# Moving the output norm of a Mamba chunk, and the start of the MLP woven into it

## The chip, the cores and the metric

The kernel runs on one core of one Trainium2 chip. The metric is the time of one execution on the device in microseconds; lower is better. The core's engines work side by side, each through its own queue of instructions in order: TensorE (PE, matrix products; PEld is its loading of weights), VectorE (DVE), ScalarE (ACT, which also evaluates functions such as exp, sqrt and silu), GpSimd (POOL) and SyncE (SP, which here issues most transfers). They meet through semaphores.

## The reference, cut to what matters

One layer for 2048 tokens of width 512, in float32: a Mamba2 mixer and a gated MLP, then a mixture of eight experts, two for each token.

```python
def mamba2(x, ...):
    z, xb, Bc, Cc, dt = split(x @ in_proj_w)
    xBC = silu(causal_depthwise_conv(cat(xb, Bc, Cc), conv_w, conv_b))
    y = ssd_chunked(x_h * dt, dt * A, B_h, C_h) + D * x_h    # chunks of 128 tokens
    y = rmsnorm(y * silu(z), norm_w)
    return y @ out_proj_w

def attn(hidden):
    h = hidden + mamba2(rmsnorm(hidden, ln1_w), ...)
    h2 = rmsnorm(h, ln2_w)
    return h + silu(h2 @ gate_w) * (h2 @ up_w) @ down_w

x = x + attn(layernorm(x))
x = x + experts(layernorm(x))      # top 2 of 8, weighted
```

## The kernel before

**Tiling.** The 2048 tokens are cut into 16 chunks of 128 (index `t`), 8 blocks `b` of two chunks, and 4 MLP blocks `fb` of two blocks each. Tokens stand on the partitions where a norm is taken, features where a product follows; `transposed` (L182) turns a tile with four PE transposes `pt` and one DVE product that reads them out (L190).

**Mamba.** `mamba(b)` (L784) is a generator: it does the two chunks of block `b` and, between their steps, what block `b+1` needs (`prepare`, and `project`: in-projection halves `pm` and `pz` of L312, convolution, silu). It yields 16 times in a chunk, 32 times in a block. `chunk(b, j, ...)` (L366) is a generator too, of which `mamba` takes eight steps in each chunk, and a ninth at the chunk's end (`yield "end"`, then `finish(pieces)`). For each half `gp` of the heads it multiplies `ec` by the channels on POOL (L378), takes scores `psc` (L383), exponentials of `cum` on ACT (L389), their products on DVE (L391), sums `py` (L406 and L414) in the only buffer of pool `ps_y`, and the new state (L421, L436). The tile `xd` (L397, one buffer) is written by DVE in the first half. `cum` comes by a broadcast transfer (L284, SP) and is masked on POOL (L286) in `spread`; `ec` by transfers of L296.

The end of a chunk is what the change touches. In step 6, `y` is squared on ACT into `sq` (L449, L450), which shares `xd`'s buffer, and summed on POOL (L452). In step 7, PE projects `y` into `po` (L457, 8 matmuls, pool `ps_mm` of two buffers), and sums the squares over the partitions (`pms`, L459). Then come the root and reciprocal `ry` (L141, L142), the normed input plus the projection `h` (L464, L465, DVE), the residual `x += h` on POOL (L466) and its store on ACT's queue (L467). The next `x` loads (L78) wait for such stores. Two empty yields follow. The ninth part squares `h` into a new tile with the sum in `m2` (L473), takes the root `r2`, multiplies (L476) and transposes the result into `h2T[fb]`, the MLP's input.

**MLP.** `feed_forward(fb)` (L670) works on 512 tokens as two halves, with seven products in place of eight: `sums` (L651) forms sums `ts` of the halves of `h2T` (L657 to L660). Each of 16 column blocks `c` has four pieces of two products `px`, `py` (L683) and two matmul groups of an earlier pair's down-projection `pd` (L667, added up by DVE in L668). ACT copies products out of PSUM (L722, L728, L735), DVE adds others (L710, L716, L742, L747), silu is in L711 and L717. A 65th piece does the last down-projections; then `route` (L550) normalises and picks experts.

**Order.** PE's instructions are placed by a tile scheduler, by priority, in blocks 0 and 1; from block 2 on they run as written. The other engines' are scheduled throughout. The driver (L833 to L854) starts the generator of `feed_forward(fb-1)` with block `2*fb` and takes one piece of it at each piece of Mamba, the 65th at the `"end"` of the second block, and a step of routing at every fourth piece. The last MLP block (`fb = 3`) runs after Mamba, and the experts last.

Of the kernel before, what the change touches and what calls it, by code (L numbers as in the profile page):

```python
# [8 lines left out]
F32 = mybir.dt.float32  # L9
I32 = mybir.dt.int32  # L10
AF = mybir.ActivationFunctionType
ALU = mybir.AluOpType
# [3 lines left out]
P = 128  # L16
T = 2048
D = 512
NK = D // P
# [5 lines left out]
NCH = TB // P  # L25
NB = T // TB
FB = 512
NFB = T // FB
# [3 lines left out]
NFC = DFF // FC  # L32
# [12 lines left out]
C_CW, C_CB, C_NW, C_D, C_L1, C_L2, C_DTB, C_AL = 0, 48, 60, 68, 76, 80, 84, 100  # L45
# [4 lines left out]
def mamba_mlp_moe(ctx, tc, x, w_in, w_out, w_gu, w_down, par, wr, wg, wu, wd, out):  # L50
# [3 lines left out]
    nc = tc.nc  # L54

    def bc(ap, axis, n):
        ap = ap.unsqueeze(axis)
        shape = list(ap.shape)
        shape[axis] = n
        return ap.to_broadcast(shape)  # L60
# [19 lines left out]
    params = pw.tile([P, NPAR], F32, name="params")  # L80
# [58 lines left out]
    def rsqrt_eps(dst, src, scale=1.0):  # L139

        nc.scalar.activation(dst, src, AF.Sqrt, bias=eps, scale=scale)  # L141
        nc.vector.reciprocal(dst, dst)  # L142
# [12 lines left out]
    wa = pa_stack.enter_context(tc.tile_pool(name="wa", bufs=2))  # L155
# [7 lines left out]
    ps_mm = psa_stack.enter_context(tc.tile_pool(name="ps_mm", bufs=2, space=PSUM))  # L163
    ps_sg = psa_stack.enter_context(tc.tile_pool(name="ps_sg", bufs=1, space=PSUM))
    ps_y = psa_stack.enter_context(tc.tile_pool(name="ps_y", bufs=1, space=PSUM))
# [3 lines left out]
    def bank(kind, shape, name):  # L169
        pool, tag = use[kind]  # L170
        return pool.tile([P, *shape], F32, name=name, tag=tag)
# [10 lines left out]
    def transposed(src, dst, weight=None):  # L182

        pt = bank("tr", [NK, P], "pt")
        for k in range(NK):
            nc.tensor.transpose(pt[:, k, :], src[:, k * P : (k + 1) * P], ident)  # L186
        if weight is None:
            nc.scalar.copy(dst, pt)
        else:
            nc.vector.tensor_tensor(dst, pt, bc(weight, 2, P), ALU.mult)  # L190
# [108 lines left out]
    def finish(steps):  # L299
        while True:  # L300
            try:
                next(steps)
            except StopIteration as end:
                return end.value
# [42 lines left out]
    def channels(b):  # L347
        xb = wa.tile([P, 4, TB], F32, name=f"xb{b}", tag="xb")
        return xb, [None, None]

    state = wa.tile([P, 2, 4, HD], F32, name="state", bufs=1)
    h2T = [None] * NFB

    def turned_x(t, xb):

        tok = slice(t % NCH * P, (t % NCH + 1) * P)
        pt = ps_tr.tile([P, 4, P], F32, name=f"ptx{t}", tag="tr")
        for m in range(4):
            nc.tensor.transpose(pt[:, m, :], xb[:, m, tok], ident)
        xbt = wa.tile([P, 2, 4, HD], F32, name=f"xbt{t}", tag="xbt")  # L360
        nc.scalar.copy(xbt.rearrange("p a g d -> p (a g d)"), pt.rearrange("p a q -> p (a q)"))
        return xbt
# [3 lines left out]
    def chunk(b, j, dt, ncum, dtdec, cd, cum, ec, xb, cs, zs):  # L366

        t = b * NCH + j
        tok = slice(j * P, (j + 1) * P)
# [3 lines left out]
        y = zs[:, :, tok]  # L373

        for gp in range(2):
# [49 lines left out]
            for i in range(4):  # L425
                at = C_D + 4 * gp + i
# [19 lines left out]
            xbts[t + 1] = turned_x(t + 1, xb if j == 0 else xc[0])  # L446

        sq = wa.tile([P, 8, P], F32, name=f"sq{t}", tag="xd", bufs=1)
        nc.scalar.activation(sq[:, 0:4, :], y[:, 0:4, :], AF.Square)  # L449
        nc.scalar.activation(sq[:, 4:8, :], y[:, 4:8, :], AF.Square)  # L450
        for n in (4, 2, 1):
            nc.gpsimd.tensor_tensor(sq[:, 0:n, :], sq[:, 0:n, :], sq[:, n : 2 * n, :], ALU.add)  # L452
        yield

        po = ps_mm.tile([P, D], F32, name=f"po{t}", tag="mm")
        for m in range(8):
            nc.tensor.matmul(po, y[:, m, :], w_o[:, m, :], start=(m == 0), stop=(m == 7))  # L457
        pms = ps_tr.tile([P, 1], F32, name=f"pms{t}", tag="tr")
        nc.tensor.matmul(pms, sq[:, 0, :], ones[:, 0:1], start=True, stop=True)  # L459

# [2 lines left out]
        h = wa.tile([P, D], F32, name=f"h{t}", tag="tok", bufs=3)  # L463
# [1 line left out]
        nc.vector.scalar_tensor_tensor(h, po, ry, h, ALU.mult, ALU.add)  # L465
        nc.gpsimd.tensor_tensor(res[t], res[t], h, ALU.add)  # L466
        nc.scalar.dma_start(out=resd[t], in_=res[t])  # L467
        yield
        yield

        h2 = wa.tile([P, D], F32, name=f"h2{t}", tag="tok", bufs=3)
        m2 = wa.tile([P, 1], F32, name=f"m2{t}", tag="m2")
        nc.scalar.activation(h2, h, AF.Square, accum_out=m2)  # L473
        r2 = wa.tile([P, 1], F32, name=f"r2{t}", tag="r2")
        rsqrt_eps(r2, m2, scale=1.0 / D)
        nc.vector.tensor_scalar_mul(h2, h, r2)  # L476
        fb, off = divmod(t * P, FB)
        if off == 0:
            h2T[fb] = (wk if fb % 2 else wa).tile([P, 2, NK, FH], F32, name=f"h2T{fb}", tag="h2T", bufs=1)
        half, off = divmod(off, FH)  # L480
        transposed(h2, h2T[fb][:, half, :, off : off + P], params[:, C_L2 : C_L2 + NK])

# [1 line left out]


    KH = NK // 2
    AT_ONCE = 400
    early_d = [scratch.tile([P, 3, KH, FC], F32, name=f"early{c}", tag=f"early{c}") for c in range(NFC)]  # L490
    late_d = [scratch.tile([P, 4, KH, FC], F32, name=f"late{c}", tag=f"late{c}") for c in range(NFC)]

# [177 lines left out]
    def feed_forward(fb):  # L670
# [20 lines left out]
        for c in range(NFC):  # L691
# [15 lines left out]
            def p2():  # L707
                product(x2, late[:, 2], b21)
                with tc.high_priority(AT_ONCE):
                    nc.vector.tensor_tensor(a[:, 0], a[:, 0], x2, ALU.add)  # L710
                nc.scalar.activation(a[:, 0], a[:, 0], AF.Silu)  # L711

            def p3():
                product(x2, late[:, 1], b22, False)
                with tc.high_priority(AT_ONCE):
                    nc.vector.tensor_tensor(a[:, 1], a[:, 1], x2, ALU.add)  # L716
                nc.scalar.activation(a[:, 1], a[:, 1], AF.Silu)  # L717

            def p5():
                product(x2, early[:, 1], t1)  # L720
                with tc.high_priority(AT_ONCE):
                    nc.scalar.copy(up, x2)  # L722
# [3 lines left out]
            product(x1, early[:, 0], b11)  # L726
            with tc.high_priority(AT_ONCE):
                nc.scalar.copy(a[:, 0], x1)  # L728
# [4 lines left out]
            product(x1, early[:, 2], t2, False)  # L733
            with tc.high_priority(AT_ONCE):
                nc.scalar.copy(a[:, 1], x1)  # L735
# [4 lines left out]
            product(x1, late[:, 0], t3, False)  # L740
            with tc.high_priority(AT_ONCE):
                nc.vector.tensor_tensor(up, up, x1, ALU.add)  # L742
# [27 lines left out]
    xc = channels(0)  # L770
    ready = None
    for pair in range(6):
# [3 lines left out]
        elif pair == 2:  # L776
            ready = finish(coming)
# [5 lines left out]

    def mamba(b):  # L784

        nonlocal ready, xc
        hT, dt, ncum, dtdec, cd, _ = ready
        xb, cs = xc
        zs = wa.tile([P, 8, TB], F32, name=f"zs{b}", tag="zs", bufs=1)
        if b + 2 < NB:  # L790
            load_x((b + 2) * NCH)
        more = b + 1 < NB
        if more:
            coming = prepare(b + 1)
            xc = channels(b + 1)
        n = 0
        for j in range(NCH):
            pieces = chunk(b, j, dt, ncum, dtdec, cd, *near[j], xb, cs, zs)
            for _ in range(4):

                if n < 2:
                    halves = (gate(b, pair, hT, zs) for pair in (2 * n, 2 * n + 1))
                elif more:
                    halves = project(b + 1, n - 2, next_hT, *xc)
                else:
                    halves = iter(())
                next(pieces)
                if more and n == 0:
                    next(coming)
                yield  # L810
                next(pieces)
                if more and n == 3:
                    next(coming)
                next(halves, None)
                yield
                if more and n < 3:
                    next(coming)
                elif more and n == 3:
                    ready = finish(coming)
                next(halves, None)  # L820
                yield
                if more and n == 0:
                    next_hT = next(coming)
                yield
                n += 1
            yield "end"
            finish(pieces)
            if j == 0 and b + 2 < NB:
                load_x((b + 2) * NCH + 1)
            if more:  # L830
                near[j] = spread(b + 1, j, ready[-1])

    BPF = FB // TB  # L833
    tail = None
    in_order = ExitStack()
    for fb in range(NFB):
        if fb == 1:

            in_order.enter_context(tc.manual_schedule(engines={mybir.EngineType.PE}))
        feed = feed_forward(fb - 1) if fb else None  # L840
        for b in range(fb * BPF, (fb + 1) * BPF):
            n = 0
            for piece in mamba(b):
                if piece == "end":
                    if feed and b % BPF == BPF - 1 and n == 16 * NCH:
                        next(feed)
                    continue
                n += 1
                if feed:
                    next(feed)  # L850
                if tail and n % 4 == 3:
                    next(tail, None)
        tail = feed
    pa_stack.close()  # L854


# [87 lines left out]
    feed = feed_forward(NFB - 1)  # L944
# [8 lines left out]
    tail = routed(tail)  # L953
# [181 lines left out]
```

## Time and profile before

| | us |
|---|---|
| runs, median (lowest to highest) | 1606.52 (1604.34 to 1612.76) |
| profiled execution | 1616.04 |
| its span, first to last instruction | 1614.1 |
| PE busy in it | 1549.4 |
| ACT table loads in it, 195 of 1.283 us | 250.2 |

The stages lie thus in the span: block 0's inputs until about 80 us, the chunks of blocks 0 and 1 without an MLP until about 216, Mamba and MLP woven together until about 1090, the last MLP until about 1255, then the experts. A row of the profile names line, engine, operation, the tile written, an arrow and the tiles read, with partitions x elements; in a timeline the brackets at the end tell how long the engine had been idle and what ended that. One fp32 matmul of the program is two records of the trace, two passes.

### The profile page before, as it was taken

To read this page: it belongs to the slowest core of one execution; us is meant where nothing else is said; L and a number is where in the kernel's file an instruction comes from. 1 tells how busy PE (TensorE), PEld (TensorE's weight loads), DVE (VectorE), ACT (ScalarE), POOL (GpSimd) and SP (SyncE) were. 2 spreads that over 40 slices of the span, in tenths; PEclk is the share of its full clock that TensorE was granted. 3 is DMA by queue.
4 is the path that set the end of the run, shared out by engine and by line. 5 is a ranking of instruction groups with operands and counts; after the bars stand their busy time and mean duration, and the time that the engine had idled before them with its cause. 6 is when DMAs were issued, how large, how long until landed. Compare 5 with 4: busy or idle time off the path is not lost. (4 is left out here: it accounts for less than half of the span.)

```text
span 1614.1 us, 18988 instructions
## 1 busy us (share of the span) xinstructions
PE 1549.4 (96%) x6283; PEld 1057.4 (66%) x6283; DVE 766.1 (47%) x2019; ACT 679.9 (42%) x1287; POOL 401.6 (25%) x486
## 2 busy tenths in 40 slices
PE   5998979999999999999999999998999999999997
PEld 4756567767676766777676677657666656666663
DVE  4785744554456557536554673444533352222221
ACT  3897875643553555246545443223122211111110
POOL 5222243342341112211221121011100113333331
PEclk9999989999999999999999999999999989999999
DMA  7553535554554543343454432237785223333332
GB/s 237 174 151 98 161 102 161 182 174 155 167 193 140 165 156 125 124 125 125 137 163 158 160 97 85 88 119 264 221 295 166 85 40 66 66 66 65 66 65 33
DMA packets 127326, 218.66 MB, mean 135 GB/s; under 512 B 11456, under 2 KB 71360, under 8 KB 127232
## 3 DMA queue, kind: packets, MB, share of 16 engines
q1 hardware_dynamic: 104960, 166.08, 33.1%
q0 software_dynamic: 8736, 20.45, 7.2%
q10 hardware_dynamic: 13536, 30.94, 5.1%
q8 instruction: 52, 0.85, 0.2%
q14 instruction: 42, 0.34, 0.1%
HBM read 176.01 MB, written 41.42 MB: 135 GB/s over the span
## 5 line engine op out<-in xcount | busy, mean ns | idle before, releaser
L667 PE MATMUL pd<-md,a 128*128 128x512 f32 x512 | 238.5, 592 | 0.0
L312 PE MATMUL pm<-hT,wi 128*128 128x256 f32 x768 | 190.9, 396 | 0.0
L312 PEld LDWEIGHTS pm<-hT,wi 128*128 128x128 f32 x768 | 147.8, 198 | 28.9 <-issue 6.9
L667 PEld LDWEIGHTS pd<-md,a 128*128 128x128 f32 x512 | 97.1, 190 | 75.4 <-issue 66.0
L668 DVE TENSOR_TENSOR r<-r,pd 128x512 f32<-128x512 f32 x128 | 87.6, 685 | 113.7 <-PE pd L667 107.8
L683 PE MATMUL py<-h2T,ms 128*128 128x256 f32 x512 | 132.4, 381 | 2.2 <-DMA ms<-late 2.2
L333 DVE SCALAR_TENSOR_TENSOR ca<-pre,params,ca 128x256 f32<-128x256 f32 x288 | 125.4, 491 | 0.4
L992 PE MATMUL epg<-ew,xgT 128*128 x312 | 120.9, 470 | 0.3 <-issue 0.2
L992 PE MATMUL epu<-ew,xgT 128*128 x312 | 120.5, 468 | 0.0
L312 PE MATMUL pz<-hT,wi 128*128 128x256 f32 x512 | 117.1, 382 | 0.2 <-DMA wi<-in_w_in 0.2
L748 POOL TENSOR_TENSOR a<-a,up 128x256 f32<-128x256 f32 x64 | 48.0, 750 | 268.8 <-DVE up L742 189.7
L457 PE MATMUL po<-w_o,zs 128*128 128x512 f32 x256 | 113.4, 594 | 0.0
L1013 PE MATMUL epd<-ew,ehT 128*128 (+1 forms) x234 | 107.2, 593 | 1.0 <-DVE ehT L1006 1.0
L683 PEld LDWEIGHTS py<-h2T,ms 128*128 128x128 f32 x512 | 96.3, 191 | 17.8 <-issue 3.0
L312 PEld LDWEIGHTS pz<-hT,wi 128*128 128x128 f32 x512 | 95.8, 191 | 14.6 <-issue 2.2
L389 ACT ACTIVATE cum<-cum,ncum 128x128 f32<-128x128 f32 x256 | 84.9, 392 | 6.0 <-POOL cum L286 3.9
L457 PEld LDWEIGHTS po<-w_o,zs 128*128 128x128 f32 x256 | 48.2, 190 | 59.1 <-issue 56.4
L716 DVE TENSOR_TENSOR a<-a,py 128x256 f32<-128x256 f32 x64 | 26.9, 421 | 124.5 <-PE py L683 105.2
L973 POOL DMA_INDIRECT xg<-xnd,idx x39 | 38.8, 995 | 185.6 <-PE pt L186 176.8
L992 PEld LDWEIGHTS epu<-ew,xgT 128*128 128x128 f32 x312 | 60.6, 194 | 34.3 <-issue 2.3
L1019 POOL DMA_INDIRECT out<-ey,idx x39 | 61.9, 1588 | 75.8 <-DVE ey L1018 39.5
L389 ACT ACT_TABLE_LOAD x59 | 75.7, 1283 | 0.9
(245 smaller groups left out, 2511.5 us busy)
## 6 DMA issues: line engine op xcount, KB each, us to landing
wi<-in_w_in SPq DMA_DIRECT2D x80, 512.0 KB, 3.9
ms<-late SPq DMA_DIRECT2D x48, 512.0 KB, 3.8
mg<-early SPq DMA_DIRECT2D x48, 384.0 KB, 3.1
md<-in_w_down SPq DMA_DIRECT2D x64, 256.0 KB, 3.7
cum<-rowsd SPq DMA_DIRECT2D x32, 512.0 KB, 4.4
late<-ms ACTq DMA_DIRECT2D x16, 512.0 KB, 3.9
ec<-rowsd SPq DMA_DIRECT2D x60, 128.0 KB, 4.1
xnd<-xn ACTq DMA_DIRECT2D x28, 256.0 KB, 4.5
```

What stands on the lines that cost most here:

```text
L312: nc.tensor.matmul(pm[:, m, :], w[:, k, m * P : (m + 1) * P], hT[:, k, :], start=(k == 0), stop=(k == NK - 1))
L333: nc.vector.scalar_tensor_tensor(ca, pre[:, m, k : k + TB], cw[:, k : k + 1], ca, ALU.mult, ALU.add)
L389: nc.scalar.activation(lt[:, half, i], lt[:, half, i], AF.Exp, bias=ncum[:, j, h : h + 1])
L457: nc.tensor.matmul(po, y[:, m, :], w_o[:, m, :], start=(m == 0), stop=(m == 7))
L667: nc.tensor.matmul(pd, a[:, j * P : (j + 1) * P], d, start=(m == 0), stop=(m == 1))
L668: nc.vector.tensor_tensor(rows[j], rows[j], pd, ALU.add)
L683: nc.tensor.matmul(ps, w[:, k], m[:, k], start=(first and k == 0), stop=(k == KH - 1), skip_group_check=True)
L748: nc.gpsimd.tensor_tensor(a[:, 1], a[:, 1], up, ALU.mult)
L973: nc.gpsimd.indirect_dma_start(out=xg, out_offset=None, in_=src, in_offset=bass.IndirectOffsetOnAxis(ap=idx[:, n : n + 1], axis=0))
L992: nc.tensor.matmul(ps, xT[:, k, :], w[:, lo : lo + EI], start=(k == 0), stop=(k == NK - 1))
L1013: nc.tensor.matmul(pd, hT[:n, m, :], w[:n, NG + m * D : NG + (m + 1) * D], start=(m == 0), stop=(m == len(ET) - 1))
L1019: nc.gpsimd.indirect_dma_start(out=out, out_offset=bass.IndirectOffsetOnAxis(ap=idx[:, n : n + 1], axis=0), in_=y, in_offset=None, compute ...
```

## The change

Four things. The squares and their sums get high priority in the scheduler. `po` goes into `y`'s bank (pool `ps_y`), and a piece later `pms` and all that follows from it. The norm of `h` follows at once in the same step: its square goes into the upper half of `sq`, and `h` is scaled in place, so that the tile `h2` is gone. The ninth part, now the transposes alone, is run in the next chunk after its second step. Then the driver: a block's MLP starts two pieces into block 2, pieces are counted in a list, so that every later MLP block starts directly after the one before (65 pieces against the chunks' 64), and what is left after the last block of Mamba runs behind it, with the last ninth part after two pieces.

```diff
--- before.py
+++ after.py
@@ -350,6 +350,7 @@
 
     state = wa.tile([P, 2, 4, HD], F32, name="state", bufs=1)
     h2T = [None] * NFB
+    AT_ONCE = 400
 
     def turned_x(t, xb):
 
@@ -446,15 +447,17 @@
             xbts[t + 1] = turned_x(t + 1, xb if j == 0 else xc[0])
 
         sq = wa.tile([P, 8, P], F32, name=f"sq{t}", tag="xd", bufs=1)
-        nc.scalar.activation(sq[:, 0:4, :], y[:, 0:4, :], AF.Square)
-        nc.scalar.activation(sq[:, 4:8, :], y[:, 4:8, :], AF.Square)
-        for n in (4, 2, 1):
-            nc.gpsimd.tensor_tensor(sq[:, 0:n, :], sq[:, 0:n, :], sq[:, n : 2 * n, :], ALU.add)
-        yield
-
-        po = ps_mm.tile([P, D], F32, name=f"po{t}", tag="mm")
+        with tc.high_priority(AT_ONCE):
+            nc.scalar.activation(sq[:, 0:4, :], y[:, 0:4, :], AF.Square)
+            nc.scalar.activation(sq[:, 4:8, :], y[:, 4:8, :], AF.Square)
+            for n in (4, 2, 1):
+                nc.gpsimd.tensor_tensor(sq[:, 0:n, :], sq[:, 0:n, :], sq[:, n : 2 * n, :], ALU.add)
+        yield
+
+        po = ps_y.tile([P, D], F32, name=f"po{t}", tag="y")
         for m in range(8):
             nc.tensor.matmul(po, y[:, m, :], w_o[:, m, :], start=(m == 0), stop=(m == 7))
+        yield
         pms = ps_tr.tile([P, 1], F32, name=f"pms{t}", tag="tr")
         nc.tensor.matmul(pms, sq[:, 0, :], ones[:, 0:1], start=True, stop=True)
 
@@ -465,20 +468,18 @@
         nc.vector.scalar_tensor_tensor(h, po, ry, h, ALU.mult, ALU.add)
         nc.gpsimd.tensor_tensor(res[t], res[t], h, ALU.add)
         nc.scalar.dma_start(out=resd[t], in_=res[t])
-        yield
-        yield
-
-        h2 = wa.tile([P, D], F32, name=f"h2{t}", tag="tok", bufs=3)
+
         m2 = wa.tile([P, 1], F32, name=f"m2{t}", tag="m2")
-        nc.scalar.activation(h2, h, AF.Square, accum_out=m2)
+        nc.scalar.activation(sq[:, 4:8, :].rearrange("p a q -> p (a q)"), h, AF.Square, accum_out=m2)
         r2 = wa.tile([P, 1], F32, name=f"r2{t}", tag="r2")
         rsqrt_eps(r2, m2, scale=1.0 / D)
-        nc.vector.tensor_scalar_mul(h2, h, r2)
+        nc.vector.tensor_scalar_mul(h, h, r2)
+        yield
         fb, off = divmod(t * P, FB)
         if off == 0:
             h2T[fb] = (wk if fb % 2 else wa).tile([P, 2, NK, FH], F32, name=f"h2T{fb}", tag="h2T", bufs=1)
         half, off = divmod(off, FH)
-        transposed(h2, h2T[fb][:, half, :, off : off + P], params[:, C_L2 : C_L2 + NK])
+        transposed(h, h2T[fb][:, half, :, off : off + P], params[:, C_L2 : C_L2 + NK])
 
 
 
@@ -486,7 +487,6 @@
 
 
     KH = NK // 2
-    AT_ONCE = 400
     early_d = [scratch.tile([P, 3, KH, FC], F32, name=f"early{c}", tag=f"early{c}") for c in range(NFC)]
     late_d = [scratch.tile([P, 4, KH, FC], F32, name=f"late{c}", tag=f"late{c}") for c in range(NFC)]
 
@@ -783,7 +783,7 @@
 
     def mamba(b):
 
-        nonlocal ready, xc
+        nonlocal ready, xc, ninth
         hT, dt, ncum, dtdec, cd, _ = ready
         xb, cs = xc
         zs = wa.tile([P, 8, TB], F32, name=f"zs{b}", tag="zs", bufs=1)
@@ -809,6 +809,8 @@
                     next(coming)
                 yield
                 next(pieces)
+                if n % 4 == 0:
+                    finish(ninth)
                 if more and n == 3:
                     next(coming)
                 next(halves, None)
@@ -823,34 +825,44 @@
                     next_hT = next(coming)
                 yield
                 n += 1
-            yield "end"
-            finish(pieces)
+            ninth = pieces
             if j == 0 and b + 2 < NB:
                 load_x((b + 2) * NCH + 1)
             if more:
                 near[j] = spread(b + 1, j, ready[-1])
 
     BPF = FB // TB
-    tail = None
+    ninth = iter(())
+    flow = []
+    tail = iter(())
+
+    def advance():
+        nonlocal tail
+        now = flow[0]
+        next(now[0])
+        now[1] -= 1
+        if now[1] % 4 == 1:
+            next(tail, None)
+        if not now[1]:
+            finish(tail)
+            tail = flow.pop(0)[0]
+
     in_order = ExitStack()
-    for fb in range(NFB):
-        if fb == 1:
+    for b in range(NB):
+        fb, at = divmod(b, BPF)
+        if fb and at == 0:
+            flow.append([feed_forward(fb - 1), 4 * NFC + 1])
+        if b == BPF:
 
             in_order.enter_context(tc.manual_schedule(engines={mybir.EngineType.PE}))
-        feed = feed_forward(fb - 1) if fb else None
-        for b in range(fb * BPF, (fb + 1) * BPF):
-            n = 0
-            for piece in mamba(b):
-                if piece == "end":
-                    if feed and b % BPF == BPF - 1 and n == 16 * NCH:
-                        next(feed)
-                    continue
-                n += 1
-                if feed:
-                    next(feed)
-                if tail and n % 4 == 3:
-                    next(tail, None)
-        tail = feed
+        for n, _ in enumerate(mamba(b)):
+
+            if b > BPF or b == BPF and n > 1:
+                advance()
+    for n in range(flow[0][1]):
+        if n == 2:
+            finish(ninth)
+        advance()
     pa_stack.close()
```

## The prediction

> **What bounds the kernel now.** I read the cores first (one core, span 1614.1 us, clock 0.984), then the busy shares, then a table by stage, then the waits of PE, then the timeline around each wait of over 1 us, and last the activation-table loads. First the busy shares and the stages:
>
> ```profile
> PE 1549.4 (96%) x6283; PEld 1057.4 (66%) x6283; DVE 766.1 (47%) x2019; ACT 679.9 (42%) x1287; POOL 401.6 (25%) x486
> ```
>
> ```profile
> 0.00:80.00 80.00, 60.70 (x262) 47.25 (x262) 49.16 (x139) 47.18 (x74) 32.71 (x55) 0.96 0.65 207
> 80.00:240.00 160.00, 142.56 (x607) 96.05 (x606) 104.99 (x284) 132.32 (x220) 47.98 (x63) 0.95 0.43 128
> 240.00:1010.00 770.00, 766.25 (x3277) 544.32 (x3276) 418.11 (x1124) 384.06 (x738) 194.10 (x254) 1.00 0.46 147
> 1010.00:1100.00 90.00, 87.66 (x321) 55.04 (x321) 40.31 (x92) 24.03 (x50) 13.48 (x15) 1.00 0.36 115
> ```
>
> The columns are the stretch, its length, the busy time of PE, PEld, DVE, ACT and POOL, PE's clock, DMA. PE is idle for 1614.1 - 1549.4 = 64.7 us in all; only that, and the slower clock in some stretches, can be won, since the change removes no matmul. In the 770 us in which Mamba and MLP run woven together, PE idles 3.75 us. The change can gain only where the weave begins (80 to 240) and ends (1010 to 1100): 17.4 + 2.3 us idle. What ends that idle time:
>
> ```profile
> PE pms L459 <- POOL sq L452: 9.8, 2, 5.6
> ...
> PE px L683 <- DVE ts L658: 3.0, 1, 3.0
> PE pc L249 <- DVE dA L246: 2.9, 2, 1.7
> ...
> PE px L683 <- ACT a L735: 2.0, 2, 1.3
> ...
> PE px L683 <- DVE h2T L190: 0.9, 1, 0.9
> ```
>
> The timeline places them (start, duration; in brackets the idle time before):
>
> ```profile
> 124.98 0.58 PE L459 MATMUL pms<-ones,sq 128*128 128x1 f32 x2 [4.20 <-POOL sq L452]
> 125.43 5.93 PE L312 MATMUL pm<-hT,wi 128*128 128x256 f32 x16
> ```
> ```profile
> 224.54 1.10 PE L683 MATMUL px<-ts,mg 128*128 128x256 f32 x4 [3.03 <-DVE ts L658]
> 225.48 1.85 PE L683 MATMUL py<-ts,mg 128*128 128x256 f32 x4
> ```
>
> So the second chunk of each of the first two blocks waits for its squares (4.20 us, and 5.59 us at 207.81), and the first MLP block waits once for its operand sums. Each wait is followed by slow matmuls: pm x16 in 5.93 us, where unhindered halves of 8 take 1.81, so 3.62; px, py and pt after the third lose some 1.3 us. One matmul of the program is two records here.
>
> **What the Trainium skill says.** "TensorE: Matmul & The Clock Gate", Part 1, says that an idle window of some 3.4 us halves PE's clock until it has been busy for as long. The trace agrees in kind: x1.64 longer after 4.20 us, nothing visible after waits of 1.2 to 1.7 us. "PSUM — Partial Sum Buffer", the four PSUM rules, says that one bank holds 512 fp32 columns; po is 128x512, so in y's only buffer it shuts out the next chunk's py until h is read out. No run so far shows po there. "ScalarE: Activation LUTs", What ACT_TABLE_LOAD costs, gives 1283 ns for a change of function set and another 1380 ns of drain. The trace has 1283, but no drain: the root of 574.95 ends at 575.24, the load begins at 575.26 and the exponential at 576.56. I price a load at 1.28 us.
>
> **The change part by part**, on the profiled execution's own time (1616.04, of which 1614.1 is the span).
>
> Squares at high priority, pms a piece behind po, in blocks 0 and 1, where a scheduler places PE's work. The stall is that of POOL's queue: at 200.02 the cum select starts after 8.04 us of waiting for its DMA, then two ec products (2.48), a state product (1.04), three square sums (2.59), and pms follows at 207.81. The new instruction order keeps the sums behind that same select. For chunk 3 it only swaps the state product with the first sum: nothing gained on POOL. On PE three matmuls of pm now precede pms: 6 x 0.226 = 1.36 us of cover, so -1.4. For chunk 1 four of eight pm matmuls go ahead (8 x 0.226 = 1.81), but the state product, so far done before the select, comes between it and the sums (+1.05): -0.8, within -1.8 to +0.5. The slow clock after both stalls stays (at best -4.2).
>
> po in y's bank. po of chunk t waits for y to be read out, which it needs anyway as its input; py of chunk t+1 waits for h, which comes 0.26 + 0.16 + 0.75 = 1.17 us plus hand-overs after pms, while at least a half of pm or an MLP product pair (1.8) stands between. 0; if the cover fails, 0.5 us in each of 16 chunks, +8.
>
> Norm of h: Square, root and product follow h at once, in place, and the transposes go after the next chunk's second call. For most chunks these lie over 10 us of PE work later: 0. But chunk 3's transposes stand close behind pms in the new order: five pm matmuls (2.3), psc (1.1), py (1.0) against a chain of 0.26 + 0.16 + 0.75 + 0.63 + 0.19 + 0.29 + 0.16 + 0.48 = 2.9 us and its hand-overs. I add +1 there (0 to +2.5). The in-place product makes DVE wait for POOL's residual sum (1.26 us beside 1.3 on ACT): 0. The Square writes into the buffer of xd, so the next xd waits for it and not for pms: DVE stands about 1 us longer behind it while MLP read-outs queue, which have 2 to 4 us of room: +0.5 in all (0 to +8). The store of the residual goes 2 to 4 us later on ACT's queue, and with it the loads of x (SP waits 91.7 us for it already); weight loads behind those have some 10 us of room: 0.
>
> MLP begun two pieces into block 2. The wait of 3.03 us and its 1.3 us of slow clock go: two pz halves and the products without sums (over 4 us) now stand before px needs them: -4.3, with +0.5 for what may be late next: -3.8. At the other end, the last MLP starts behind five leftover pieces instead of one; the three after the transposes hold some 9 us of PE work with their down products, so 0.94 goes wholly and most of 1.31 (the copy L735): -1.9. The pc wait (1.25 and 1.67) loses nothing certain: dA comes about 1 us earlier, and pc now comes ahead of po: 0 (-1 to +3).
>
> Table loads. The new order of ACT, whose loads it lists, has 237 where the trace before has 195 (59 at L389, 29 at L141, 28 at L717, 22 at L339, 21 at L345, 36 elsewhere). By chunk 3's ry there are 9 fewer (54 against 63), so 11.5 us less in a stretch where ACT is 83% busy; from there to chunk 13's ry 51 more (168 against 117), 38 of these in chunks 9 to 13. The MLP's activations, three pieces shifted against the chunk, fall singly between exponentials. 51 x 1.28 = 65 us raise ACT from 384 to some 449 of 770 us, 58%: no bound. What may hurt is a load ahead of a copy that empties a PSUM bank (L722, L728, L735). Before, about 117 loads in that stretch go with 2.3 us of PE waits for ACT (1.6 xT, 0.7 a), 0.02 each; 51 more at twice that: +2 (0 to +33, the latter at half of every load).
>
> Sum: -1.4 - 0.8 + 1 + 0.5 - 3.8 - 1.9 + 2 = -4.4, so the profiled execution would take 1611.6. The median shown (1606.52) lies 9.5 under the profiled one; I carry the difference over: 1602.1, and say 1602.
>
> **The rivals.**
>
> A, the stalls at the start go altogether. For it: ACT has 11.5 us less to do there, and if its exponentials come earlier, cum's buffers and the selects do too. Against it: the DMA that the select waits for is released by PE's py (SP, L296 before L284). It would give another 9.8 + 4.2 - 1.4 - 0.8 = 11.8 in gain: 1590.
>
> B, table loads push PSUM copies onto PE's path. Place: chunks 8 to 13, at L722, L728 and L735, with 0.9 to 2.7 us of room now. Price: 0.5 us of PE for each of 38 loads, 19 us in place of 2. For it: the loads stand directly ahead of such copies, and ACT's queue is in order. Against it: 117 loads cost nearly nothing. It gives -4.4 - 2 + 19 = +12.6: 1619. It turns the sum's sign from 0.17 us a load, and passes +8 from 0.38.
>
> C, xd behind the Square, or py behind h, costs half a microsecond a chunk: +8 in place of 0.5, so +3.1: 1610. For it: DVE already stood 61.1 us before xd. Against it: PE idled 0.5% of that stretch all the same.
>
> That the change doesn't do what it says: the new order shows po, pms, transposes and MLP moved as told. Excluded.
>
> **How the numbers follow.** Forecast 0.50, A 0.18, B 0.20, C 0.12. The forecast's own range is 1593 to 1609 (clock recovery on one side, chunk 3's transposes and loads on the other). Half a per cent, some 8 us, is about what a measurement of this kernel tells from no change: 1598.5 and 1614.5 are the bounds. Faster: A's 0.18 and 0.19 of the forecast's lower part, 0.37. Slower: B's 0.20 and 0.04 of C, 0.24. Same: 0.39. The range of 8 in 10 reaches from A's middle past B's lower half: 1588 to 1617.
>
> **What would show it.** pms after sq: 3.4 and 4.2 us if I am right, gone if A holds. At the first px<-ts no wait of 3 us. PE's idle time between 240 and 1010: under 8 us if right; over 20 with px or py released by a copy of ACT's if B holds; py L406 or L414 waiting for h, or px for a DVE product behind xd, if C. Loads: 237. Wrong I would be if PE's stalls at the start follow ACT and not POOL, or if the weave has less room for late copies than its single waits suggest.

## The result, and the profile after

The changed kernel takes 1603.45 us in the median of 20 runs against 1611.26 for the kernel before beside it: ratio 0.9951, 95% interval 0.9939 to 0.9963, so 8 us faster. (The 1606.52 given above for the kernel before is the median of its first three runs.) The profiled execution took 1599.17 us, with a span of 1597.4, which is 16.7 under the span before. The traces show where a good part of the difference between 8 and 16.7 comes from. The first expert product (`epg`) starts at 1264.39 us before and at 1252.99 after, 11.4 earlier. The experts, whose code is the same, then take 349.7 us before and 344.4 after: PE's idle time there is nearly equal (16.4 and 16.2 us), its recorded clock 0.97 and 0.98. So 5.3 us of the difference of the spans is how PE's clock fell in these two executions, and not the change.

The busy shares of the changed kernel:

```profile
PE 1539.3 (96%) x6283; PEld 1050.6 (66%) x6283; DVE 769.4 (48%) x2019; ACT 729.7 (46%) x1329; POOL 395.8 (25%) x486
```

As many matmuls as before take 10 us less, at a mean clock of 0.991 in place of 0.984. ACT works 49.8 us more, on 42 more instructions, all table loads (237 for 195). The same stages as before (stretch, length, busy PE, PEld, DVE, ACT, POOL, PE's clock, DMA):

```profile
0.00:80.00 80.00, 59.29 (x260) 46.78 (x261) 49.13 (x144) 46.46 (x76) 32.91 (x54) 0.96 0.65 207
80.00:240.00 160.00, 151.89 (x663) 101.33 (x661) 109.70 (x290) 123.14 (x217) 52.89 (x67) 0.98 0.43 133
240.00:1010.00 770.00, 763.97 (x3249) 541.64 (x3249) 419.40 (x1117) 447.68 (x789) 185.41 (x251) 1.00 0.45 147
1010.00:1100.00 90.00, 88.25 (x351) 58.60 (x350) 40.92 (x93) 23.84 (x53) 12.21 (x15) 1.00 0.46 147
```

Between 80 and 240 us PE idles 8.1 us in place of 17.4, at a clock of 0.98 in place of 0.95. In the weave from 240 to 1010 it idles 6.0 in place of 3.75, so there the change costs a little. PE's waits after (waiting engine, line, what it waited for: us in all, times, longest):

```profile
PE pms L462 <- POOL sq L454: 4.3, 2, 3.3
...
PE pn L258 <- ACT ry L141: 3.2, 5, 1.1
PE pt L186 <- DVE h L476: 2.8, 2, 1.8
...
PE py L683 <- ACT up L722: 2.1, 2, 1.4
...
PE pc L249 <- DVE dA L246: 0.9, 1, 0.9
```

The wait of `px` for `ts` is no longer listed, `pms` waits 4.3 us in place of 9.8 and `pc` 0.9 in place of 2.9. New are `pn` behind `ry` and `pt` behind `h`. The place of the first stall, in PE's timeline after:

```profile
113.75 2.32 PE L312 MATMUL pm<-hT,wi 128*128 128x256 f32 x10
...
117.21 6.17 PE L459 MATMUL po<-w_o,zs 128*128 128x512 f32 x14
124.43 0.38 PE L462 MATMUL pms<-ones,sq 128*128 128x1 f32 x2 [1.05 <-POOL sq L454]
124.67 1.97 PE L312 MATMUL pm<-hT,wi 128*128 128x256 f32 x8
```

`pms` of chunk 1 comes at nearly the same time as before (124.43 and 124.98), because POOL's sums do. But PE has done 8 records of `pm` more by then, and after a wait of 1.05 us the rest run at full speed: 8 records in 1.97 us, where before 16 took 5.93 after 4.20 us of waiting. The gain here is the work in front and the clock behind, not the time of `pms`. In chunk 3 `pms` does come earlier (203.38 in place of 207.81), because POOL's select there starts at 195.44 in place of 200.02.

### The profile page after: what moved, and what is told of

Read it like the earlier page. It is cut to its first block, busy times and chain, and to the rows that moved or that the text cites. A ratio compares the mean times of both kernels' runs of the same rounds, so it can differ in the third digit from the quotient of the medians.

```text
span 1597.4 us, 19066 instructions
## 1 busy us (share of the span) xinstructions
PE 1539.3 (96%) x6283; PEld 1050.6 (66%) x6283; DVE 769.4 (48%) x2019; ACT 729.7 (46%) x1329; POOL 395.8 (25%) x486
## 5 line engine op out<-in xcount | busy, mean ns | idle before, releaser
L748 POOL TENSOR_TENSOR a<-a,up 128x256 f32<-128x256 f32 x64 | 47.7, 745 | 299.3 <-DVE up L742 232.6
L728 ACT COPY a<-px 128x256 f32<-128x256 f32 x64 | 23.6, 369 | 131.7 <-PE px L683 113.0
L188 ACT COPY xgT<-pt 128x512 f32<-128x512 f32 x39 | 22.7, 586 | 126.0 <-PE pt L186 126.0
```

Of the source, the lines that this page charges most:

```text
L748: nc.gpsimd.tensor_tensor(a[:, 1], a[:, 1], up, ALU.mult)
```

## The experiments

Each was timed in five rounds beside the kernel before; ratios are to it. "Weave" is the stretch from 240 us to chunk 15's `pms`; there PE idles 3.8 us before and 6.0 in the changed kernel. The last two columns are read from one profiled execution of each kernel. The changed kernel and e11 are the same program, and differ there by 0.3 and 2.3 us.

| | what | ratio (95%) | idle in the weave, us | first `epg` at, us |
|---|---|---|---|---|
| before | | 1 | 3.8 | 1264.4 |
| changed | | 0.9951 (0.9939 to 0.9963) | 6.0 | 1253.0 |
| e1 | new chunk, old driver | 0.9998 (0.9984 to 1.0013) | 11.2 | 1265.4 |
| e2 | old chunk, new driver | 1.0053 (1.0037 to 1.0070) | 10.7 | 1269.3 |
| e3 | MLP's phase kept | 1.0031 (1.0016 to 1.0045) | 14.6 | 1268.4 |
| e4 | `po` in the pool of `pm` | 1.0018 (1.0004 to 1.0032) | 8.4 | 1267.8 |
| e5 | e3, routing moved by a piece | 0.9925 (0.9902 to 0.9947) | 5.5 | 1256.8 |
| e6 | more table loads | 0.9956 (0.9940 to 0.9973) | 9.5 | 1254.8 |
| e7 | `pms` not delayed | 0.9928 (0.9902 to 0.9953) | 3.2 | 1251.0 |
| e8 | `pms` in the pool of `pm` | 0.9937 (0.9916 to 0.9958) | 2.9 | 1253.3 |
| e9 | e5 and e7 | 0.9916 (0.9898 to 0.9935) | 2.1 | 1248.9 |
| e10 | e9, PE adds squares | 0.9898 (0.9881 to 0.9914) | 1.8 | 1244.3 |
| e11 | changed, again | 0.9951 (0.9933 to 0.9969) | 5.7 | 1250.7 |

**e1: the chunk alone.** The changed `chunk` with `mamba` and the driver of before, so that the ninth part runs at the chunk's end:

```diff
-            ninth = pieces
+            yield "end"
+            finish(pieces)
```

> The changed chunk (squares at high priority, po in y's bank, pms a piece behind, norm of h in place) with the driver of before: ninth part at the chunk's end, MLP started with block 2's first piece; 204 table loads. Theory: the gain before the weave (pms waits of 9.8 us fall to some 4, less slow clock behind them) is this part's, the wait of px for ts (3.0 us and 1.3 of slow clock) stays: 4 to 6 us under before, ratio to before 0.996 to 0.9975. Rival, the later MLP start made the whole gain: within 1.5 us of before.

Neither: no gain at all, though the stalls of `pms` shrank (4.5 us, chunk 3's at 198.88 us in place of 207.81). PE's timeline of e1:

```profile
198.88 0.38 PE L463 MATMUL pms<-ones,sq 128*128 128x1 f32 x2 [2.06 <-POOL sq L455]
199.12 4.09 PE L312 MATMUL pm<-hT,wi 128*128 128x256 f32 x10
...
217.28 2.04 PE L684 MATMUL px<-ts,mg 128*128 128x256 f32 x4 [6.30 <-DVE ts L659]
219.12 1.91 PE L684 MATMUL py<-ts,mg 128*128 128x256 f32 x4
```

Of the 8.9 us by which chunk 3's `pms` comes earlier, about a third is lost at the next place: `ts` needs the transposes and the sums of DVE, and PE now arrives sooner. The wait is 6.30 us where it was 3.03, with slow matmuls behind it, and the mean clock from 198.88 to 240 us is 0.83. At this `px` e1 is still 7.3 us ahead (217.28 against 224.54), and at the last `pz` before 240 us 5.9 (234.77 against 240.69). The weave takes the rest, with 7.4 us more of idle time: `px` waits for the last product of the piece before (L748, 4.1 us) and for a copy of ACT's (L736, 2.2).

**e2: the driver alone.**

```diff
-                if n % 4 == 0:
-                    finish(ninth)
...
-            ninth = pieces
+            finish(pieces)
```

with the `chunk` of before.

> The chunk of before, with the new driver: MLP begun two pieces into block 2, phase drifting by a piece with each MLP block; 257 table loads. Theory: pms waits stay at 9 to 10 us, the 3.0 us at px<-ts goes, loads cost about 2: 2 to 4 us under before, ratio 0.9975 to 0.999. Rival, the loads matter (62 more at 0.3 us or more): 10 us or more over before. Rival, the MLP start makes the whole gain: 7 to 8 us under before.

8 us slower than before. The wait for `ts` went, and 2.9 us of a wait for `hn` came in its place (223.94 us). `pms` waits 9.6 us as before. In the weave the transposes wait for `h` (3.3 us), `po`, `pl` and a down product for a read-out of DVE (2.2), and `px` for the last product of the piece before (L747, 1.9). Neither half of the change gains alone; the two together do.

**e3: the phase of the MLP kept.** Every later MLP block's first piece is taken in the same slot as the last piece of the one before:

```diff
             finish(tail)
             tail = flow.pop(0)[0]
+            if flow:
+                advance()
```

> The changed kernel, but each later MLP block's first piece is taken together with the last piece of the one before, so that the phase against the chunks stays that of block 2; 214 table loads in place of 237. Theory, the extra loads are nearly hidden: within 2 us of the changed kernel (ratio to before about 0.995), PE's waits for ACT in the weave at 2 to 5 us. Rival, loads push copies onto PE's path: 5 us or more faster than the changed kernel, ratio to before 0.992 or less.

Neither: 23 table loads fewer, and 13 us slower than the changed kernel by the ratios. PE's waits in e3's weave say where:

```profile
PE pl L571 <- DVE r L668: 6.2, 8, 0.8
...
PE pc L249 <- ACT xT L188: 1.4, 2, 0.7
PE psum L266 <- ACT xT L188: 1.4, 2, 0.7
```

and PE's timeline shows the pattern that comes back eight times:

```profile
559.80 1.99 PE L312 MATMUL pm<-hT,wi 128*128 128x256 f32 x8
561.63 1.03 PE L683 MATMUL px<-ts,ms 128*128 128x256 f32 x4
562.49 1.88 PE L667 MATMUL pd<-md,a 128*128 128x512 f32 x4
565.15 1.06 PE L571 MATMUL pl<-wr_sb,xT 128*128 128x8 f32 x8 [0.78 <-DVE r L668]
...
567.84 1.33 PE L312 MATMUL pm<-hT,wi 128*128 128x256 f32 x5
```

`pm` is one accumulation in two halves (559.80 and 567.84). As long as it is open, it holds one of the two buffers of its pool. `pd` takes the other, and the routing's `pl`, which uses the same pool, waits until DVE has read `pd` out. Whether a routing step falls between the halves or behind them depends on the MLP's phase; the constant phase put all of them between.

**e5: e3 with routing a piece earlier.**

```diff
-        if now[1] % 4 == 1:
+        if now[1] % 4 == 0:
             next(tail, None)
```

> The steady phase of e3, with the routing steps one piece earlier (when remaining pieces leave 0, not 1, by four), so that they fall behind the second half of a pm and not between its halves; 219 loads. Theory: e3 lost by routing's pl waiting for the down-projection's read-out (8 x 0.78 us) and by transposes against pc and psum (4 x 0.68), because an open pm holds one of two buffers: these 9 us go, PE idles 4 to 6 us in the weave, ratio to before 0.993 to 0.996. Rival, the constant phase itself is bad: stays at 1.001 or more.

0.9925: 17 us faster than e3 by the ratios, from routing one piece earlier. The first `epg` comes 11.5 us earlier, the weave's idle time is down by 9.2 us, and `pl` and the waits for `xT` are gone from its list. So it was not the phase, but where it put the routing. That e5 beats the changed kernel is not shown: their intervals overlap, and in the profiles its first `epg` comes later (1256.8 against 1253.0, and 1250.7 in e11).

**e4: `po` back in the pool of `pm`.**

```diff
-        po = ps_y.tile([P, D], F32, name=f"po{t}", tag="y")
+        po = ps_mm.tile([P, D], F32, name=f"po{t}", tag="mm")
```

> The changed kernel with po back in the two-buffer pool that pm and pz use. Theory: held a piece longer there, po leaves pm and pz one buffer, and PE waits for their read-out in each chunk, 0.3 to 0.7 us: 5 to 10 us slower than the changed kernel, ratio to before about 1.000. Rival, the bank makes no difference: within 2 us of the changed kernel, ratio 0.995.

11 us slower than the changed kernel, but in another place than expected. Before the weave, in e4:

```profile
126.79 0.38 PE L462 MATMUL pms<-ones,sq 128*128 128x1 f32 x2 [3.72 <-POOL sq L454]
127.03 5.39 PE L312 MATMUL pm<-hT,wi 128*128 128x256 f32 x16
```

Here the whole last `pm` stands behind `pms` again, and the slow clock with it: `pms` waits 8.7 us in all. With `po` in `y`'s bank a buffer is free in `pm`'s pool, and the scheduler takes half of that `pm` ahead (the timeline of the changed kernel above). Between 80 and 240 us e4 idles 7.6 us more than the changed kernel, in the weave only 2.4 us more.

**e7: `pms` in the same piece as `po`.**

```diff
             nc.tensor.matmul(po, y[:, m, :], w_o[:, m, :], start=(m == 0), stop=(m == 7))
-        yield
         pms = ps_tr.tile([P, 1], F32, name=f"pms{t}", tag="tr")
...
         nc.vector.tensor_scalar_mul(h, h, r2)
         yield
+        yield
```

> The changed kernel with pms, h and its norm in the same piece as po (an empty piece takes the place of the other yield); po still in y's bank; 224 loads. Theory: PE has 3 to 4 matmuls of pm less between po and pms in chunks 1 and 3, so pms waits 2 to 3 us longer in all, with 1 to 2 us of slow clock; the waits of pn for ry (3.2 us) and of pt for h (2.8 us) go: within 3 us of the changed kernel, ratio 0.993 to 0.997. Rival, the delay makes the gain: 5 us or more slower, ratio 0.998 or more.

The ratio is at the low end of what the theory gave, but only one of its terms came as told: `pn` no longer stands directly behind `pms` for the transposes' one bank, and its 3.2 us went. `pms` waits 4.9 us, as long as in e11, with half of chunk 1's `pm` still ahead, and `pt` still waits 2.8 us for `h`. So the piece between `po` and `pms` brings nothing measurable. Whether 0.9928 is faster than the changed kernel stays open, since the intervals overlap.

**e8: `pms` in the pool of `pm`.** The same `ps_tr` to `ps_mm`, for `pms`.

> The changed kernel with pms in the two-buffer pool of pm and pz instead of the transposes' single bank, where pn follows it; 243 loads. Theory: the 3.2 us of pn waiting for ry go and nothing takes their place: 2 to 3 us faster than the changed kernel, ratio 0.993 to 0.994. Rival, pms then holds a buffer that pm needs: 3 us or more slower, ratio 0.997 or more.

`pn`'s 3.2 us went, and 1.2 us of `pm` waiting for a read-out came. Before the weave `po` now waits 2.7 us for DVE, which the theory did not have. The ratio is where the theory put it, but its interval takes in the changed kernel, and the first `epg` comes no earlier (1253.3).

**e6: more table loads.**

```diff
+                if fb < NFB - 1:
+                    root = small_p.tile([P, 1], F32, name=f"root{fb}_{c}", tag="root")
+                    nc.scalar.activation(root, a[:, 1, 0:1], AF.Sqrt, bias=eps, scale=0.0)
                 nc.scalar.activation(a[:, 1], a[:, 1], AF.Silu)
```

in the first three MLP blocks.

> The changed kernel with a root of one column put ahead of one silu in each column block of the first three MLP blocks: 48 small activations, 282 table loads in place of 237. Theory, loads in the weave cost PE almost nothing (0.02 to 0.1 us each): 1 to 5 us slower than the changed kernel, ratio to before 0.996 to 0.998. Rival B of the prediction, 0.5 us for each load: 22 us slower, ratio 1.009.

ACT is busy 500.9 us from 240 to 1010, 53 more than in the changed kernel. PE idles 3.5 us more in the weave, under 0.1 us for each of 45 loads, and the ratio moves by 0.0005, within its interval; at the interval's upper end, 0.9973, it would be 3.5 us, again under 0.1 us for each. Rival B would have needed 1.009. These loads stand ahead of a silu, not directly ahead of a copy out of PSUM, so B's own place is tested only in so far as the copies stand behind them in ACT's queue.

**e9 and e10: what is left.** e9 joins e5 and e7. In e10, POOL does only the first of three sums of squares in chunks 1 and 3:

```diff
-            for n in (4, 2, 1):
+            for n in (4,) if t in (1, 3) else (4, 2, 1):
...
+        left = 4 if t in (1, 3) else 1
+        for m in range(left):
+            nc.tensor.matmul(pms, sq[:, m, :], ones[:, 0:1], start=(m == 0), stop=(m == left - 1))
```

> The edits of e5 (steady phase, routing behind the second half of pm) and e7 (pms in the same piece as po) together; 223 loads. Theory, both take out waits of different places, pn for ry (3.2 us) and those of the drifting phase: the weave's idle time falls to 3 or 4 us, ratio to before 0.991 to 0.993, 3 to 5 us under the changed kernel. Rival, each only reshuffles the small waits: ratio 0.994 to 0.996.

> e9, and in chunks 1 and 3 POOL does only the first of the three square sums while PE adds the other four slices with three more one-column matmuls in pms. Theory, POOL's queue ends both waits: each pms comes about 1.3 us earlier for 0.7 us more of PE, so the two waits of 4.9 us fall to some 2.3 and the slow clock behind them with it: 1 to 3 us faster than e9. Rival, the waits there are ended by something else than the sums: no change, or 1 us slower.

> The changed kernel itself, beside e9 and e10 on the same chip: ratio to before 0.994 to 0.996, as before.

All three are at or a little better than the theory's numbers; e9 and e10 still overlap. In PE's timeline of e10:

```profile
197.92 1.05 PE L463 MATMUL pms<-ones,sq 128*128 128x1 f32 x8 [1.04 <-POOL sq L454]
198.84 2.40 PE L312 MATMUL pm<-hT,wi 128*128 128x256 f32 x10
```

The wait is 1.04 us in place of 3.33 in e9 and 3.27 in the changed kernel, and the ten records behind it take 2.40 us in place of 3.62 and 4.09. Only the shorter wait is sure: in e11 the ten records take 2.41 us behind a wait of 3.28 (the last section has the lines). e10 is the fastest kernel here: 0.9898, with the interval of the changed kernel beside it (0.9933 to 0.9969) wholly above its own.

## Why the prediction was right, step by step

The forecast of 1602 us, 4.4 under its base, met a change of 8 us in the same direction and of about twice its size. That 1602 lies so close to the measured 1603.45 is luck: the base of 1606.52 was 4.7 us under the median of the twenty runs, and the gain came out 3.4 us larger than forecast, so the two errors nearly cancel. The place of the gain, the start of the weave, was right. The terms did not all hold.

- **Waits of `pms`.** Forecast -2.2 us, with the slow clock staying; measured -5.5 us of waiting (-4.9 in e11), 3.2 in chunk 1 and 2.3 in chunk 3, and the clock behind chunk 1's `pms` is back. Two things were off. In chunk 1 I left out that POOL may start earlier: the state product did come ahead of the sums (1.09 us), but the select before it began at 116.42 us in place of 117.82, because its transfer had landed sooner; chunk 3's select, too, began sooner, by 4.6 us. And I put the cover down to the delay of `pms`; e4 and e7 show that most of it comes from `po`'s new bank, which I priced at nothing.
- **Start of the MLP.** Forecast -3.8 us; the wait of 3.03 us is gone and the three groups behind it run at full speed. Right. But e1 and e2 show that this term and the last one can't be added one by one: with the MLP's old start, what is won at `pms` is lost again at `ts` and in the weave.
- **`pt` behind `h`.** Forecast +1 us; measured +2.8, in chunks 1 and 3. I had missed chunk 1.
- **End of the weave.** Forecast -1.9 us; the waits of 2.25 us before (1090 to 1096 us) stand as 1.76 after (1080 to 1087 us), now for `r` and two copies. About -0.5: new waits took the old one's place.
- **`pc`.** Forecast 0, measured -2.0, within the bounds given.
- **Table loads.** Forecast 237 and +2 us; 237 they were, and e6 bounds them at under 0.1 us each. The mechanism of B, a load in front of a copy, was not what the weave's 2.3 us came from: the one long wait for a copy (`py` for L722, 1.38 us at 256.23) has no load ahead of the copy, but 3.90 us in which ACT stood for POOL. It shows only at the end of the weave, where a load stands shortly ahead of both copies, for 0.26 and 0.72 us.
- **The weave.** Forecast +2.5 (loads, and `xd` behind the Square), measured +2.3; that the sizes agree is luck, for the main cause is another: `pn` takes the transposes' bank right behind `pms` and waits for `ry`, five times, up to 1.06 us when ACT loads a table in between. e7 and e8 each took it out. `py` behind `h` is in no list of the changed kernel's waits, and the one wait of `px` for a product of DVE in the weave (0.5 us at 531.74) has no `xd` ahead of it, so C did not happen.

These waits sum to -5.9 us, and the idle time up to the first `epg` fell by 6.4; the other 5.0 us up to there are clock. Part of that is chance: up to the first `epg` the profiles record 30.7 us of half clock before, 17.1 in the changed kernel and 10.2 in e11, which is the same program. Rival A, the stalls gone altogether, came about in part: half the waiting, and the clock behind one of two (behind both in e11). What stays open: the high priority of the squares was not tried alone, nor was the norm of `h` in place, and why e1's weave idles 11 us is read from its waits only.

## What to carry to other kernels

When one engine is busy 96% of the time, a stall taken out can come back at the next places where the operands are just in time (in e1 all of it did, a third of it at the very next one), so move those places along with it, and test the parts together as well as alone. Where PE's order is written by hand, ask of each small step which PSUM buffer it takes and which accumulation is open at that moment; one piece earlier or later was worth 17 us here by the ratios (e3 against e5). A gain in PE's clock behind a wait should be read from more than one execution. Table loads on an engine with room to spare were the largest visible number in the change and cost almost nothing.

## What the runs showed of the hardware

The profiles record the clock that PE is granted. It is full or half, and half clock comes in stretches of 3.413 us, or of two or three times that. Within one execution the starts of these stretches lie whole multiples of 3.413 us apart (139.22, 204.07 and 1122.26 us in the changed kernel).

The length of a wait alone does not decide whether half clock follows. This is chunk 3 in two executions of the same program, first the changed kernel, then e11:

```profile
203.38 0.38 PE L462 MATMUL pms<-ones,sq 128*128 128x1 f32 x2 [3.27 <-POOL sq L454]
203.62 4.09 PE L312 MATMUL pm<-hT,wi 128*128 128x256 f32 x10
```
```profile
203.54 0.38 PE L462 MATMUL pms<-ones,sq 128*128 128x1 f32 x2 [3.28 <-POOL sq L454]
203.79 2.41 PE L312 MATMUL pm<-hT,wi 128*128 128x256 f32 x10
```

The clock is 0.50 from 204.07 to 207.48 us in the first, and 1.00 over the same records in the second. One `pls` of the routing beside the last MLP (L648, at 1121.53 us in the changed kernel) waits 2.16 or 2.17 us in all thirteen profiles. Half clock follows in nine of them (its 8 records take 3.04 us in the changed kernel) and not in the other four (1.97 us in e11). In e1 a wait of 2.06 us was enough (ten records in 4.09 us).

What counts is how the idle time falls on the steps of 3.413 us. Between 60 us and 10 us before the end, the thirteen profiles have 5742 such steps at full clock. All 37 in which PE idled more than 2.02 us were followed by half clock, and none of the 5615 in which it idled less than 1.1 us; between these, 19 of 90. So the prediction's measure, a wait of some 3.4 us, was too simple. A wait of 1.04 or 1.05 us cost nothing visible beyond itself here. Waits of 3.27 and 3.28 us at chunk 3's `pms` cost next to nothing more (ten records in 2.41 us, where 2.26 is unhindered), 1.8 us (4.09) or 2.3 us (4.61 in e5 and e7), depending on where they fell. After 4.20 us sixteen records took 5.93, which is 2.3 us over their unhindered 3.62.
